# Conditioning rows in quarter strips, and a new order of loads and gathers in the opening of a conditioned block

## The chip, the cores and the metric

The kernel runs on one core of a Trainium2 chip (trn2). The core has five engines that run side by side: PE (TensorE, matrix products into PSUM), DVE (VectorE), ACT (ScalarE), POOL (GpSimd) and SP (SyncE, which here only issues transfers). Semaphores order them; sixteen DMA engines move data. The metric is the device time of one execution in microseconds (us); less is better.

## The reference, cut to what matters

x has 32 rows of 128 tokens with 512 features, fp32. `t` holds one conditioning vector of 512 per row, and `mask` marks the last tokens of each row (at most 32 of 128).

```python
m = mask[:, :, None]
emb = silu(t) @ ada_w + ada_b                      # 512 -> 3 * 512
shift, scale, gate_msa = split(emb, 3)
norm = where(m, layernorm(x) * (1 + scale[:, None]) + shift[:, None], 0)
fwd = gelu(norm @ ssm_w1 + ssm_b1) @ ssm_w2 + ssm_b2
bwd = gelu(norm @ bwd_w1 + bwd_b1) @ bwd_w2 + bwd_b2     # the two flips cancel
x = x + gate_msa[:, None] * where(m, fwd + bwd, 0)
shift_mlp, scale_mlp, gate_mlp = split(silu(t) @ ffada_w + ffada_b, 3)
h = gelu_tanh((layernorm(x) * (1 + scale_mlp) + shift_mlp) @ ff_w1 + ff_b1)   # 512 -> 1024
out = x + gate_mlp[:, None] * (h @ ff_w2 + ff_b2)
```

The first half (the lines with ssm and bwd) changes only masked tokens; the second half runs over all 4096.

## The kernel before, in words

**First half, over slots.** The masked tokens are numbered, and the first 512 become slots, four tiles of 128. `find_slots` (products with `rank` at L238, then DVE) gives the token of every slot, `gather` (L254) fetches the tokens' rows of x into `xc[0]` to `xc[3]` by indirect transfers on POOL. `pick` is a 0/1 matrix of batch rows by slots, repeated in four strips of 32 partitions. A tile goes through `statistics` (L155, with a root on POOL), `modulated` (L182, L183), four transposes on PE (L190), eight blocks f of the hidden layer (L582 for the first tiles, L199 for the rest; f0 to f3 use ssm_w1, f4 to f7 bwd_w1), and `project` (L216) with w2. `finish_slots` (L320 to L324) writes the new rows of tiles 0 and 1 to `x1_wide` in DRAM, with their own mean and root. Tiles 2 and 3 follow later as `xn_late`, `xT_t`, hidden "s1", and projections s2 and s3.

**Conditioning.** `modulation_matmuls` (L279) multiplies silu(t), transposed (`sT`, 512 by 32), with `ada_a` in four blocks k of 128 rows. The results for shift, scale and gate lie in three strips of 32 partitions (one batch row each) and 512 columns. The gate's own product is made as four partial strips (`gate_strips`, L541), copied by ACT, and added up by one product with `strips` (L550); L541 then runs once more, as `pm_keep_clock`, and its result is not used. `of_slots` (L299) spreads a kind from batch rows to a slot tile by a product with `pick`; its output is 128 by 512 in one PSUM bank. `keep_gate` copies gates to SBUF. The second half's conditioning is `pm_f` from `ada_f`, transposed into `modT` (L727).

**Second half, over all tokens.** 32 tiles in four pairs of sides, each side four tiles. For the first pair, `raw[0]` to `raw[3]` (two tiles each) hold x; `own_statistics` (L168 to L172) computes mean and root; `take_first_half` (L752) overwrites the rows that the first half changed, by eight indirect transfers from `x1_wide` with out-of-range indices skipped. `normalised_of_side_0` and DVE's 32x32 transposes make side 0 ready for `turned` (L832, transfers that finish the transpose); `normalised_of_side_1` makes four tiles for `turn(0)` to `turn(3)` (PE transposes at L821, DVE L813). Both products of the second half use Strassen's scheme with seven products on halves, at two levels; `weight_sums` (L639) and `combine` (L342) make the sums of weight blocks, `token_sums` (L922 to L932) those of activations. PE's products are at L993 (first layer) and L1180 (second layer).

**Order.** From L384 on all five engines run in program order. SP issues nearly all loads (its queue is in order too); POOL issues indirect ones; ACT issues a few. `load_behind_gathers` (L134) puts a one-element memset on POOL ahead of a load, so that SP issues that load only once POOL has issued what stands before the memset. Around the change PE's order is: pm_ss for k = 0 to 2, find_slots(1), pm_ss for k = 3, L541, L299, L550, L541, transposes, hidden. PSUM has pools ps_t (two banks), ps_h (three) and ps_o (three); a tile of a pool waits for the last reader of the tile whose bank it takes. `after` (L1252 to L1262) lists what is put behind which hidden block of "s1"; `put` does the same in the second half.

## Time and profile before

| what | value |
|---|---|
| runs | 463.61, 465.93, 467.93 us, median 465.93 |
| profiled execution | 468.7 us, span 467.0 us |
| busy: PE, DVE, ACT, POOL | 450.4, 339.2, 176.7, 156.3 us |
| mean granted clock of PE | 0.992 |
| DMA | 70.95 MB, 152 GB/s over the span |
| loads of the opening in SP's order | ada_a 4 x 512 KB, ada_a gates 1 MB, w1 2 x 1 MB, raw 4 x 512 KB, w2 2 x 1 MB, biases, fw1 2 MB, ada_f 4 x 768 KB |
| fw2 (2 MB) | issued by SP at 96.94 us |

The profile is of one execution. Its page gives the busy time of each engine, of 40 equal slices, the chain of waits that ended last, and groups of instructions by line; the trace behind it can be asked for the timeline or for the busy time in any stretch. PE's weight loads are a row of their own (PEld) and overlap its products. An fp32 product is recorded as two instructions, so a count of eight is four products.

### The profile page before, as it was taken

What the parts mean: (1) busy time and instruction counts of PE and PEld (TensorE: products, weight loads), DVE (VectorE), ACT (ScalarE), POOL (GpSimd) and SP (SyncE); (2) the same over time, 40 slices, a digit from 0 to 9 for tenths busy, and PEclk for the clock granted to TensorE, in tenths of its full rate; (3) what the DMA queues carried; (4) which work ended last, traced back from release to release, by engine and by line L of the source; (5) the groups of instructions that cost most, each with busy time, mean ns of one, the idle gap of its engine ahead of it and who ended that gap; (6) DMA issues with size and microseconds to landing.
All of it is one profiled execution on the core that took longest, in us unless ns stands there. A gap on an engine that the chain in (4) does not pass through costs nothing.

```text
span 467.0 us, 5898 instructions
## 1 busy us (share of the span) xinstructions
PE 450.4 (96%) x2034; PEld 366.2 (78%) x2034; DVE 339.2 (73%) x549; ACT 176.7 (38%) x381; POOL 156.3 (33%) x147
## 2 busy tenths in 40 slices
PE   6799999999899999999999999999999999999995
PEld 2186467578688888888888888888888887888884
DVE  4688767879979857996687389967873986433645
ACT  3032023544255173254544623544546144562000
POOL 4220052038774000289720004897000025660000
PEclk9799999999999999999999999999999999999999
DMA  7999336984404661934067429330773342213022
GB/s 278 363 392 392 134 76 113 340 302 175 157 1 185 98 125 41 341 111 162 3 208 103 96 78 331 108 136 2 221 107 80 125 168 80 79 66 116 0 79 105
DMA packets 82755, 70.95 MB, mean 152 GB/s; under 512 B 63136, under 2 KB 63664, under 8 KB 81698
## 3 DMA queue, kind: packets, MB, share of 16 engines
q1 hardware_dynamic: 67874, 58.47, 39.9%
q0 software_dynamic: 4064, 10.54, 6.3%
q10 hardware_dynamic: 10784, 1.52, 2.2%
q8 instruction: 17, 0.28, 0.2%
q14 instruction: 16, 0.13, 0.1%
HBM read 56.84 MB, written 13.70 MB: 151 GB/s over the span
## 4 chain that ended last, share of the span: by engine, by line
PE 75%; DVE 9%; DMA 4%; SPq 4%; ACT 3%; POOL 3%; issue 2%; ACTq 0%; DVEq 0%; POOLq 0%
PE a_o L1180 17%; PE a_m L993 15%; PE e_o L1180 13%; PE e_m L993 12%; PE po_s L216 6%; PE ph_s L199 5%; SPq L832 3%; DMA ada_a<-in_L_cond_ada_w_dram 3%; PE part_s L299 2%; DMA xT<-xn 1%; DVE sx L922 1%; ACT xT L815 1%; PE ph_s L582 1%; DVE t L342 1%; PE pm_f L279 1%
## 5 line engine op out<-in xcount | busy, mean ns | idle before, releaser
L1044 POOL TENSOR_TENSOR ha<-p_m,ha 128x512 f32<-128x512 f32 x20 | 25.8, 1290 | 176.4 <-ACT ha L1051 167.2
L1180 PE MATMUL e_o<-fw,ha 128*128 128x256 f32 x256 | 57.9, 379 | 0.0
L815 ACT ACTIVATE xT<-xT,modT 128x128 f32<-128x128 f32 x112 | 44.2, 479 | 33.3 <-DMA xT<-xn 31.0
L1180 PE MATMUL a_o<-t,hb 128*128 128x256 f32 x240 | 54.1, 379 | 0.0
L1180 PEld LDWEIGHTS e_o<-fw,ha 128*128 128x128 f32 x256 | 48.6, 190 | 6.6
L1180 PEld LDWEIGHTS a_o<-t,hb 128*128 128x128 f32 x240 | 45.6, 190 | 6.2
L955 ACT ACTIVATE hb<-hb,biasT 128x256 f32<-128x256 f32 x64 | 29.0, 500 | 28.9 <-POOL hb L1077 19.4
L1007 ACT COPY p_m<-e_m 128x512 f32<-128x512 f32 x27 | 15.8, 586 | 49.8 <-PE e_m L993 49.8
L1044 POOL TENSOR_TENSOR hb<-p_m,hb 128x512 f32<-128x512 f32 x20 | 29.3, 1467 | 1.5 <-DVE hb L1023 1.2
L752 POOL DMA_INDIRECT x<-x_rows,slot_i x24 | 27.6, 1150 | 6.3 <-issue 5.4
L1180 PE MATMUL a_o<-fw,ha 128*128 128x256 f32 x128 | 29.0, 380 | 0.0
L1180 PE MATMUL e_o<-fw,s 128*128 128x256 f32 x128 | 28.9, 379 | 0.0
L1180 PE MATMUL a_o<-t,s 128*128 128x256 f32 x128 | 28.9, 379 | 0.0
L1051 ACT COPY ha<-e_m 128x512 f32<-128x512 f32 x32 | 18.5, 579 | 25.8 <-PE e_m L993 25.3
L216 PE MATMUL po_s<-w,h_s 128*128 128x512 f32 x64 | 28.3, 592 | 0.0
L1180 PEld LDWEIGHTS a_o<-fw,ha 128*128 128x128 f32 x128 | 24.2, 190 | 3.5 <-ACT a_o L1119 0.2
L1180 PEld LDWEIGHTS e_o<-fw,s 128*128 128x128 f32 x128 | 24.3, 190 | 3.3
L1180 PEld LDWEIGHTS a_o<-t,s 128*128 128x128 f32 x128 | 24.3, 190 | 3.3
L955 ACT ACTIVATE ha<-e_m,biasT 128x256 f32<-128x256 f32 x48 | 20.1, 469 | 16.0 <-PE e_m L993 14.9
L1018 DVE TENSOR_TENSOR e_m<-a_m,ha 128x512 f32<-128x512 f32 x20 | 13.9, 696 | 16.4 <-POOL ha L1044 6.6
L993 PE MATMUL e_m<-s,fw 128*128 128x256 f32 x92 | 23.8, 382 | 1.0 <-DVE e_m L1018 1.0
L993 PE MATMUL a_m<-xT,tw 128*128 128x256 f32 x96 | 24.6, 379 | 0.0
(228 smaller groups left out, 896.4 us busy)
## 6 DMA issues: line engine op xcount, KB each, us to landing
tw<-t_rows SPq DMA_DIRECT2D x16, 896.0 KB, 4.6
x<-in_x_dram SPq DMA_DIRECT2D x16, 512.0 KB, 6.4
gate<-gate_rows POOLq DMA_DIRECT2D x8, 1024.0 KB, 5.1
out_dram<-x SPq DMA_DIRECT2D x15, 512.0 KB, 3.3
xT<-xn SPq DMA_DIRECT2D x92, 64.0 KB, 2.3
fw<-in_L_cond_ff_w_dram SPq DMA_DIRECT2D x2, 2048.0 KB, 15.4
ada_f<-in_L_cond_ffada_w_dram SPq DMA_DIRECT2D x4, 768.0 KB, 16.6
ada_a<-in_L_cond_ada_w_dram SPq DMA_DIRECT2D x4, 512.0 KB, 3.6
```

Of the source, the lines that this page charges most:

```text
L199: nc.tensor.matmul(ph[:, :n], w[:, k, ts(f, P)], xT[:, k, :], start=(k == 0), stop=(k == KC - 1))
L216: nc.tensor.matmul(po, h[f][:, ts(i, P)], w[:, f, :], start=(f == 0), stop=(f == HC - 1))
L752: nc.gpsimd.indirect_dma_start(out=raw[i // 2][:, i % 2] if p == 0 else xs[i // G][i % G // 2][:, i % 2], out_offset=None, in_=x1_rows if ...
L815: nc.scalar.activation(out, src, AF.Identity, bias=shift, scale=scale)
L832: queues[(b + q // 2) % len(queues)].dma_start(dst[ts(q, R), b], src[ts(b, R), q])
L955: nc.scalar.activation(dst[:, n], src[:, n], AF.Gelu_apprx_tanh, bias=biasT[:, f : f + 1])
L993: nc.tensor.matmul(bank[:, ts(n, QT)], self.w_block(j, product)[:, ts(n, P)], self.x_block(j, product), start=(product in ("P1", "P5") and ...
L1007: nc.scalar.copy(p5, e)
L1018: nc.vector.tensor_tensor(e, a, p5, add)
L1044: nc.gpsimd.tensor_tensor(self.place(RESULT[j], c), self.p5[j], other, ALU.add)
L1051: nc.scalar.copy(self.place(RESULT[j], c), src)
L1180: nc.tensor.matmul(part, src[:, k, ts(i, P)], w[product][:, k, :], start=(last and k == 0), stop=True, skip_group_check=True,)
```

## The change

It has five parts.

1. **Strips by quarter of the features.** The conditioning is laid out with the four strips of 32 partitions as four quarters j of 128 features, and shift, scale and gate side by side in each (`mod1`, `mod2`: 128 by 3 by 128). `modulation_matmuls` runs four products per block k, each with as many columns as kinds times 128. `of_slots` yields four banks, one for each quarter, for one or more slot tiles and kinds. `modulated_by_strips` therefore runs eight DVE instructions of 128 columns in place of two of 512. `gates_of_slots` makes all four tiles' gates at once, with four ACT copies. The bias loads become one of 64 KB for each kind, in rows of 512 bytes.
2. **Opening order.** ada_a's gate columns load behind the second gather; the first part of w1 between the two; the bias of shift and scale between ada_a's blocks 1 and 2; raw[2] and raw[3] behind fw1. The gate's products run behind the first tile's hidden blocks, f0 to f3 of both tiles are run tile by tile, and the own statistics of raw[0], raw[1] and of raw[2], raw[3] move to two later places.
3. **PE fed in the opening.** Four bf16 products of zeros at the start, and products into `pm_keep_clock` after the blocks k = 0 and 1 and after the first `of_slots`.
4. **Second-layer weights.** fw2 is loaded in eight parts, each behind one gather of `take_first_half(0)`; combine(0, 1) of fw2 runs on POOL behind weight_sums(4).
5. **Smaller moves.** token_sums(1, 0) and (1, 1) run ahead of the first product; fw1's combines are split around finish_slots(0); gate_rows is written by four transfers; some small tiles move to another SBUF pool. The loop for masked tokens beyond the slots is changed in the same manner.

```diff
+    def load_ada(t, w, blocks, width):
+
+        for k in blocks:
+            nc.sync.dma_start(t[:, k, :width], w[ts(k, P), :width])
+
+    def load_conditioning_bias(t, vec, kinds, queue):
+
+        rows = vec.rearrange("(m j c) -> m j c", m=3, c=P)
+        for m in kinds:
+            queue.dma_start(t[:, m], rows[m].unsqueeze(1).to_broadcast([KC, B, P]))
...
+    ada_a = adap.tile([P, KC, 3 * D], F32, tag="ada", name="ada_a")
+    load_ada(ada_a, ada_w, range(2), 2 * D)
+    load_conditioning_bias(modb_a, ada_b, range(2), nc.sync)
+    load_ada(ada_a, ada_w, range(2, KC), 2 * D)
...
     def modulation_matmuls(pm, ada, lo, hi, blocks):
+        kinds = ada.rearrange("p k (m d) -> p k m d", d=D)
         for k in blocks:
-            for j in range(lo, hi):
+            for j in range(KC):
                 nc.tensor.matmul(
-                    pm[ts(j, B), :],
+                    pm[ts(j, B), : (hi - lo) * P],
                     sT[:, k, :],
-                    ada[:, k, ts(j, D)],
+                    kinds[:, k, lo:hi, ts(j, P)],
                     start=(k == 0),
                     stop=(k == KC - 1),
                 )
 
     def modulation_rows(pm, mod, modb, lo, hi):
-        rows = slice(lo * B, hi * B)
-        nc.vector.tensor_tensor(mod[rows], pm[rows], modb[rows], ALU.add)
...
+        view = pm[:, : (hi - lo) * P].rearrange("p (m c) -> p m c", c=P)
+        nc.vector.tensor_tensor(mod[:, lo:hi], view, modb[:, lo:hi], ALU.add)
+
+    def of_slots(picked, tiles, mod, kinds, banks, name):
+
+        n = kinds.stop - kinds.start
+        t = [
+            pool.tile([P, 512], F32, tag=tag, name=f"{name}_{j}")[:, : len(tiles) * n * P].rearrange(
+                "p (a m c) -> p a m c", m=n, c=P
+            )
+            for j, (pool, tag) in enumerate(banks)
+        ]
+        for at, c in enumerate(tiles):
+            for j in range(KC):
+                nc.tensor.matmul(
+                    t[j][:, at],
+                    picked[ts(j, B), ts(c, P)],
+                    mod[ts(j, B), kinds],
+                    start=True,
+                    stop=True,
+                )
+        return t
...
+
+    def modulated_by_strips(src, strips, at, t, mean, rstd):
+
+        for j in range(KC):
+            nc.vector.scalar_tensor_tensor(
+                t[:, ts(j, P)], src[:, ts(j, P)], mean, strips[j][:, at, 1], ALU.subtract, ALU.mult
+            )
+        for j in range(KC):
+            nc.vector.scalar_tensor_tensor(
+                t[:, ts(j, P)], t[:, ts(j, P)], rstd, strips[j][:, at, 0], ALU.mult, ALU.add
+            )
+        return t
...
+
+    def gates_of_slots(tiles):
+
+        strips = of_slots(
+            pick, tiles, mod1, slice(2, 3), 2 * [(ps_o, "o")] + 2 * [(ps_t, "tr")], f"gate_s{tiles[0]}"
         )
...
-        return t
+        t = ssm.tile([P, len(tiles), D], F32, tag="gs", name=f"gs_{tiles[0]}")
+        for j in range(KC):
+            nc.scalar.copy(t[:, :, ts(j, P)], strips[j][:, :, 0])
+        return [t[:, n] for n in range(len(tiles))]
...
-        def combine(self, *which):
+        def combine(self, *which, engine=nc.vector):
 
             for j in which:
                 out, x, y = self.sums[j]
-                nc.vector.tensor_tensor(out, x, y, ALU.subtract)
+                engine.tensor_tensor(out, x, y, ALU.subtract)
...
+    zeros = tp.tile([P, 512], BF16, tag="t", name="zeros")
+    nc.vector.memset(zeros, 0.0)
+    pm_keep_clock = ps_h.tile([P, 512], F32, tag="h", name="pm_keep_clock")
+    for _ in range(4):
+        nc.tensor.matmul(pm_keep_clock, zeros[:, :P], zeros, start=True, stop=True)
...
-    broadcast_rows(modb_a, ada_b, nc.scalar)
...
+    load_conditioning_bias(modb_a, ada_b, (2,), nc.scalar)
...
-    gather_slots(find_slots(0))
+    token_i = find_slots(0)
+    both = xp.tile([P, 2, D], F32, tag="x", name="xc_0")
+    xc += [both[:, c] for c in range(2)]
+    gather(xc[0], token_i[:, 0:1])
     load_behind_gathers(w1[:, :, :D], ssm_w1)
-    load_behind_gathers(w1[:, :, D:], bwd_w1)
+    gather(xc[1], token_i[:, 1:2])
+    load_behind_gathers(ada_a[:, :, 2 * D :], ada_w[:, 2 * D :])
+    load_blocks(w1[:, :, D:], bwd_w1)
     raw = [x_tile(2 * n, 2) for n in range(2 * G // 2)]
     x_of = {0: [[t[:, :, :D] for t in raw[2 * side : 2 * side + 2]] for side in range(2)]}
-    for n, t in enumerate(raw):
-        nc.sync.dma_start(t[:, :, :D], x[2 * n : 2 * n + 2].rearrange("b s d -> s b d"))
+
+    def load_raw(n):
+        nc.sync.dma_start(raw[n][:, :, :D], x[2 * n : 2 * n + 2].rearrange("b s d -> s b d"))
+
+    load_raw(0)
+    load_raw(1)
     load_blocks(w2[:, :KC], ssm_w2)
     load_blocks(w2[:, KC:], bwd_w2)
...
-    mod1 = const.tile([3 * B, D], F32, name="mod1")
-    nc.vector.tensor_scalar(modb_a[B : 2 * B], modb_a[B : 2 * B], 1.0, None, ALU.add)
+    mod1 = const.tile([P, 3, P], F32, name="mod1")
+    def keep_clock(n, k):
+        for _ in range(n):
+            for j in range(KC):
+                nc.tensor.matmul(
+                    pm_keep_clock[ts(j, B), : 2 * P],
+                    sT[:, k, :],
+                    ada_a[:, k, ts(j, 2 * P)],
+                    start=True,
+                    stop=True,
+                )
+
     pm = ps_o.tile([P, 512], F32, tag="o", name="pm_ss")
-    modulation_matmuls(pm, ada_a, 0, 2, range(KC - 1))
+    for k in range(KC - 1):
+        modulation_matmuls(pm, ada_a, 0, 2, (k,))
+        if k < 2:
+            keep_clock(1, k)
     token_i = find_slots(1, (ps_h, "h"))
     modulation_matmuls(pm, ada_a, 0, 2, range(KC - 1, KC))
+    nc.vector.tensor_scalar(modb_a[:, 1], modb_a[:, 1], 1.0, None, ALU.add)
     modulation_rows(pm, mod1, modb_a, 0, 2)
...
+    strips = of_slots(pick, (0, 1), mod1, slice(0, 2), 3 * [(ps_o, "o")] + [(ps_h, "h")], "part_s0")
+    keep_clock(3, 0)
...
+    xn_s = []
+    for c in range(2):
+        mv, rstd = statistics(xc[c : c + 1], f"s{c}")
+        if c == 0:
+            gather_slots(token_i)
+        xn_s.append(modulated_by_strips(xc[c], strips, c, xn[:, c], mv[:, 0, 0:1], rstd))
...
+    load_raw(2)
+    load_raw(3)
+    ada_f = adap.tile([P, KC, 3 * D], F32, tag="ada", name="ada_f")
+    modb_f = adap.tile([P, 3, P], F32, tag="modb", name="modb_f", bufs=1)
+    load_ada(ada_f, ffada_w, range(KC), 3 * D)
+    load_conditioning_bias(modb_f, ffada_b, range(3), nc.sync)
...
+        if c == 0 and f % 2 == 0:
+            t = ps_h.tile([P, 512], F32, tag="h", name=f"ph_s0_{f}")
+            for n in range(2):
+                ph_s[f + n] = t[:, ts(n, NH)]
...
-    hidden_of_tile(0, 0)
-    hidden_of_tile(1, 0)
+    for f in range(KC):
+        hidden_of_tile(f, 0)
     transposed_slots(xn_s[1], xT_s[:, :, ts(1, P)], "s1")
-    hidden_of_tile(2, 0)
+    pm = ps_o.tile([P, 512], F32, tag="o", name="pm_g")
+    modulation_matmuls(pm, ada_a, 2, 3, range(KC))
+    modulation_rows(pm, mod1, modb_a, 2, 3)
...
+    totals = const.tile([P, 2], F32, name="totals")
+    nc.vector.tensor_copy(totals, pt[:, :2])
...
-    for n, t in enumerate(raw):
-        own_statistics(t, 2, f"x_{n}")
...
-    for f in range(3):
+    for f in range(KC):
         hidden_of_tile(f, 1)
...
+        for done in (f - 1, f) if f % 2 else ():
+            t = ssm.tile([P, NH], F32, tag="h", name=f"h_s0_{done}", bufs=HC)
+            nc.scalar.activation(t, ph_s[done], AF.Gelu, bias=biasT[:, done : done + 1])
+            h1.append(t)
...
+    gs = gates_of_slots(range(NC))
+    strips = of_slots(
+        pick, (2, 3), mod1, slice(0, 2), 3 * [(ps_o, "o")] + [(ps_t, "tr")], "part_s2"
+    )
+    xn_late = [
+        modulated_by_strips(
+            xc[2 + c], strips, c, spare[1][:, c], mv_t[:, c, 0:1], rstd_t[:, c : c + 1]
         )
-
-    gs = []
-    gate_and_next_tile(0)
+        for c in range(2)
+    ]
+    for n in range(2):
+        own_statistics(raw[n], 2, f"x_{n}")
+    h1 += hidden(xT_s, NH, w1, 0, AF.Gelu, "s0", ssm, range(KC, HC - 1))
...
+    for c in range(2):
+        with_gated_bias(c, gs[c])
...
-    h1 += hidden(xT_s, NH, w1, 0, AF.Gelu, "s0", ssm, range(3, HC - 1))
-    gate_and_next_tile(1)
-    Weights(fw1, KC // 2, FF // 2, t_1).combine(0, 1, 2, 3)
-    with_gated_bias(1, gs[1])
+    fw1_of = Weights(fw1, KC // 2, FF // 2, t_1)
     h1 += hidden(xT_s, NH, w1, 0, AF.Gelu, "s0", ssm, range(HC - 1, HC))
+    fw1_of.combine(0, 1)
     finish_slots(0, h1, gs[0])
+    fw1_of.combine(2, 3)
     t = in_blocks(group_of_tiles("tw_3"))
     t_sum[3] = [t[:, :4], t[:, 4:]]
     weight_sums(3)
     store_weight_sums(3)
-    nc.vector.tensor_scalar(modb_f[B : 2 * B], modb_f[B : 2 * B], 1.0, None, ALU.add)
...
-    mod2 = const.tile([3 * B, D], F32, name="mod2")
-    pm = ps_o.tile([P, 512], F32, tag="o", name="pm_f")
+    nc.vector.tensor_scalar(modb_f[:, 1], modb_f[:, 1], 1.0, None, ALU.add)
+    mod2 = const.tile([P, 3, P], F32, name="mod2")
+    pm = ps_h.tile([P, 512], F32, tag="h", name="pm_f")
     modulation_matmuls(pm, ada_f, 0, 3, range(KC))
     modulation_rows(pm, mod2, modb_f, 0, 3)
+    for n in range(2, 4):
+        own_statistics(raw[n], 2, f"x_{n}")
...
+        for m in range(2):
+            nc.tensor.transpose(ptr[:, ts(m, P)], mod2[:, m], ident)
+        nc.vector.tensor_copy(
+            modT.rearrange("p k (m b) -> p m k b", b=B),
+            ptr[:, : 2 * P].rearrange("p (m k b) -> p m k b", m=2, b=B),
+        )
...
+            if behind:
+                behind(i)
...
-    take_first_half(0, x_of[0], range(2 * G))
+    def load_fw2_part(k):
+        load_behind_gathers(fw2[:, k : k + 1], ff_w2[ts(k, P)])
+
+    take_first_half(0, x_of[0], range(2 * G), load_fw2_part)
...
-    nc.gpsimd.dma_start(gate_rows, mod2[2 * B : 3 * B, :])
+    for j in range(KC):
+        nc.gpsimd.dma_start(gate_rows[:, ts(j, P)], mod2[ts(j, B), 2])
...
+    def combine_behind_weight_sums():
+        done = stp.tile([1, 1], F32, tag="done", name="done", bufs=1)
+        nc.gpsimd.tensor_copy(done, t_sum[4][1][0:1, 2, 0:1])
+        fw2_of.combine(0, 1, engine=nc.gpsimd)
...
-    after[0] = [second_gates, transposed_modulation]
+    after[0] = [transposed_modulation]
...
+        combine_behind_weight_sums,
...
-    nc.sync.dma_start(fw2, ff_w2.rearrange("(k p) f -> p k f", p=P))
+    for n in range(2):
+        now.token_sums(1, n)
...
-    for n in range(2):
-        now.token_sums(1, n)
...
-            put(4, 1, fw2_of.combine, 0)
-            put(4, 3, fw2_of.combine, 1)
```

## The prediction

> **What bounds the kernel now.** I read the busy times by stretch first, then the chain of waits, then the timeline where PE is not full. In the stretches the columns are the stretch, then busy time (and count) of PE, PE's weight loads, DVE, ACT and POOL, the granted clock, the DMA share and GB/s.
>
> ```profile
> 0.00:24.60 24.60, 17.44 (x64) 5.75 (x65) 13.00 (x36) 4.91 (x8) 8.15 (x21) 0.86 0.91 325
> 24.60:92.00 67.40, 67.39 (x290) 42.78 (x291) 54.31 (x107) 19.35 (x41) 14.05 (x16) 1.00 0.71 237
> 92.00:131.00 39.00, 35.17 (x157) 28.93 (x156) 34.88 (x53) 15.26 (x31) 25.07 (x20) 1.00 0.57 202
> 131.00:386.00 255.00, 254.92 (x1179) 222.91 (x1178) 197.00 (x298) 116.28 (x259) 86.99 (x72) 1.00 0.46 129
> ```
>
> PE is full from 24.6 to 92 and from 131 to 386 us. It idles 7.2 us in the opening, 3.8 between 92 and 131, and 5.5 after 386, which the change does not touch. So there is something to win in three ways: an earlier first hidden-layer product, less PE work, and the 3.8 us. The chain of waits (start, us, what) shows the opening:
>
> ```profile
> 3.15 11.86 DMA ada_a<-in_L_cond_ada_w_dram
> ...
> 15.14 1.06 PE pm_g L541 x8
> 16.20 3.71 PE part_s L299 x8
> ...
> 24.61 2.02 PE ph_s L582 x16
> ```
>
> The scale and shift rows are done at 13.4, but their spreading to slots (L299) stands in PE's queue behind pm_g, which waits for the last part of ada_a. PE then runs at half clock (mean 0.54, 0.50, 0.50, 0.75 in the 2 us stretches from 16 to 24). The next lines are POOL's and PE's timeline (start, us, instruction, idle before and its releaser):
>
> ```profile
> 62.84 1.24 POOL L752 DMA_INDIRECT x<-x_wide,slot_i  x1 [3.76 <-DMA x_wide<-t_s]
> ...
> 72.57 1.00 POOL L752 DMA_INDIRECT x<-x_wide,slot_i  x1 [0.30 <-issue]
> ...
> 118.78 4.10 DVE L342 TENSOR_TENSOR t<-fw 128x1024 f32<-128x1024 f32 x1
> ...
> 123.54 1.13 PE L993 MATMUL a_m<-xn_sy,tw 128*128 128x256 f32 x4 [2.24 <-DVE hb L1023]
> ```
>
> Eight gathers 1.39 us apart fill side 1's tiles. DVE has the last one normalised at 76.2, and PE starts turn(0) at 76.56, just in time. The combine at 118.78 takes 4.10 instead of 1.22 us and leaves PE idle for 2.24.
>
> **What the Trainium skill says.** "TensorE: Matmul & The Clock Gate", Part 1: the clock halves after an idle window of 3.4 us and returns after a busy one. The trace agrees: pm_ss's first eight records take 3.41 us and four later ones 1.05, so full rate came near 9.7; half follows from 16.1 after a stretch with little work, and full near 23, about two windows apart each. Its Part 3: matmuls in different row or column groups run together. Agrees: pm_g's four of 512 take 1.06 us together, where L216's single ones take 0.86 each. "SBUF — State Buffer", Who interferes with whom: a DVE instruction with two SBUF inputs is locked out while a GpSimd instruction reads SBUF. Agrees: the 4.10 us combine ends at 122.88, one run of 1.22 after the tensor_tensors that POOL began at 119.32 and 120.54 (until 121.79).
>
> **The change part by part.** *Opening.* Each pm_ss block drops from 0.85 us (two 512-wide matmuls together) to 0.43 (four 256-wide). Two bias loads go into SP's queue before ada_a's blocks 2 and 3: two issues at 0.5 us (L119's 0.34 to 0.58 each) and 128 KB, 0.35 us at 370 GB/s. In exchange ACT's queue carries 64 KB instead of 192 KB, so I cost the landing at nothing; the cover for the issues is that DMA is busy with blocks 0 and 1 (1 MB, 2.8 us) meanwhile, and without it up to 1.3 us goes onto the first product. L531 no longer holds DVE for the bias (1.1 us), so rows are done at 12.5. The strips follow at once: 8 matmuls, 0.45 us for each slot tile, ready at 13.3. The first gather took 6.5 us to land beside saturated DMA; with ada_a's last 1 MB moved behind it I take 4.5 (bounds 2.7, the gathers of 62 us, and 6.5), so 12.3. Statistics cost 1.05 (12.5 to 13.6). The two 512-wide products (1.63 us for both) become eight of 128. Nearest row: L813, 128x128 from PSUM, 8 in 2.63 us, 0.33 each; bounds 0.25 and 0.40. That is 2.7, so xn_s0 at 16.5 instead of 19.9. From there to the first hidden product were 1.35 us (23.23 to 24.58): **17.9 instead of 24.6**. The four zero matmuls lie before the mask lands (2.8) and cost nothing. keep_clock(1, k) lies before block 2's landing (9.98; up to 0.85 each if that comes sooner), keep_clock(3) (1.3 us) before 16.5. Whether the clock holds is open: 0 to 1.7 us.
>
> *Loads.* The bytes are the same, the order is new. ada_a's gate part (1 MB) now follows the second gather and w1's first half on SP: at 370 GB/s from 9.4, with two gathers (0.5 MB) beside them, it lands near 18, and pm_g reads it at 22.4. Raw tiles 2 and 3 go behind fw1, so w2, the biases and fw1 land 2.7 us sooner; the tiles land before 45 and are read at 57. Cover gone, each would stop PE or DVE for its own lateness; 4 to 12 us of room make me take nothing.
>
> *PE up to the projection.* Before: 17.5 us from 24.6 to 42.1. After: hidden f0 to f3 for both tiles, 8 x 0.99 = 7.9; transposes 0.6; pm_g moved here 1.1; counts 0.1; gates (16 matmuls of 128, four together) 1.1. Then a new wait: part_s2 needs two of ps_o's three banks and one of ps_t's that the gates fill, so PE stands until ACT has copied three gate strips (three of L309's 0.59, behind two Gelus of 0.48), with its own 0.9 some 2.8 together. Hidden f4 to f7: 7.1. Sum 20.7, so projection at 38.6: the lead shrinks from 6.7 to 3.5. Queued behind the waiting matmuls are those four hidden blocks, and DVE waits for the strips. Then pm_f falls from 3.56 to 2.6, the second gates (1.91) go, ptr_mod loses 0.25. PE reaches turn(0) at **70.4 instead of 76.6**.
>
> *DVE and the gathers.* DVE has no such lead. It idles until the strips (29.2), then: late tiles 6.2 with the banks' waits; two own statistics 3.6 (1.81 each); b2 0.7; two gated biases 2.9; counts 1.4; combine(0,1) 2.5; finish 0 2.5; combine(2,3) 2.5; weight sums 2.2; finish 1 2.5. That ends at 56.2, where before it was 58.4. Then modb_f and rows 0.7 and, new ahead of the gathers, the statistics of raw tiles 2 and 3, 3.6, whose root POOL must do before its gathers: 61.4 instead of 62.84 (x_wide lands earlier, 60.7). Between gathers POOL now has a memset (0.23 at L135): 1.58 apart, the eighth at 72.5. It needs 4.0 to turn(0) as before, plus 0.6 for 2 MB of fw2 beside it (bounds 0 and 3.8, the opening's landing). **turn(0) at 77.1 instead of 76.6.** SP issues the first half's turned rows behind the eight weight parts, at 74.4 instead of 72.1; ACT's 83.2 becomes 85.5, and PE needs the first scaled halves (88.7) only after 92, which covers it by 3.3 us. The weight sums' six stores follow on SP, 2.3 later too, against a first read of t_rows at 94.85. gate_rows becomes four issues (2.3 us of POOL), covered by POOL's idle time to 99. Moving token sums costs nothing: DVE idles from 94.4 to 96.6.
>
> *Clock.* PE idles 6.7 us before turn(0). That holds a whole idle window, so about 3.4 us of busy work runs at half rate: **+1.7** (0 to 2.6).
>
> *92 to 131.* The combine on DVE goes to POOL (two of 1024, about 2.5 each, from L1044's 1.27 for 512). POOL is free at 80 to 85, where DVE reads PSUM, and its next operation with two SBUF inputs comes at 86. PE's 2.24 goes, and most of 0.58 and 0.96 with the two token sums moved ahead: **-3.3** (-1.5 to -3.8).
>
> **Sum:** +0.5 + 1.7 - 3.3 = -1.1 us. The profiled execution took 468.7 (span 467.0); the median of the runs is 465.93, so 464.8.
>
> **Rivals.** *The lead gets through:* strips at 0.25 each and the first gather early (16.5 for the first product) start the gathers 2.7 earlier, memsets hide in the 0.30 issue gap (1.39 apart), turn(0) at 72.5 and no half clock: -4.1 - 3.8 = -7.9, 458. For it: every row I took is the dearer of two; against: L813 is the same shape from PSUM. *Slower:* fw2's parts between the gathers. 256 KB more every 1.58 us makes some 328 GB/s, near the opening's 325 to 400, where gathers took 6.5 us. Then turn(0) comes at 80.6 (+4.1), the clock costs 2.6, fw2 lands late, and POOL's combine locks DVE out, leaving only -1.5: +5.2, 471.1. It decides from a landing of about 6 us. Against: it is under the highest rate seen. *The array is not kept at work:* half clock through the first hidden products as from 16 to 23 before; 1.7 more on the DVE chain and turn(0), 466.5.
>
> **Numbers.** Gathers bind, as summed: 0.44, own range 460.6 to 470.0 (ends of turn(0) -1.5 to +3, clock and 92 to 131). Lead gets through 0.32; slower 0.19; clock not held 0.05. A measurement here tells about 1% from no change: 461.3 and 470.6. Of the first case 0.05 lies below 461.3. Faster 0.37, same 0.44, slower 0.19. The range 457 to 472 takes in the rivals' centres.
>
> **What would show it.** First hidden product near 18; ACT's three copies before part_s2 on PE; DVE full from 29 to 61; gathers 1.6 apart; PE idle 5 to 7 us before turn(0), then 0.5 clock; no wait at the old combine. I am wrong if PE does not wait at turn(0), or if gathers land after 6 us.

## The result, and the profile after

| | before | after |
|---|---|---|
| median of 20 runs each | 465.48 us (463.61 to 469.18) | 466.50 us (465.15 to 467.88) |
| ratio after to before | | 1.0009, 95% interval 0.9988 to 1.0031 |
| profiled execution, its span | 468.7, 467.0 us | 467.88, 466.2 us |
| busy PE, DVE, ACT, POOL | 450.4, 339.2, 176.7, 156.3 us | 451.3, 334.5, 175.4, 164.3 us |

The interval of the ratio takes in 1: no change that can be measured. The 20 runs of before fall into two groups, 12 from 463.61 to 465.93 us and 8 from 467.93 to 469.18, with the profiled execution (468.7) at the level of the second, while the runs of after all lie between 465.15 and 467.88, the profiled one being the slowest; so these two profiles are compared with each other first, and with others further below.

After, busy time by stretch (columns as in the prediction: PE, PE's weight loads, DVE, ACT, POOL with counts, granted clock, DMA share, GB/s), with two more stretches:

```profile
0.00:24.60 24.60, 21.27 (x170) 12.36 (x174) 13.04 (x48) 4.71 (x8) 8.04 (x21) 1.00 0.88 313
24.60:92.00 67.40, 61.92 (x316) 40.22 (x305) 51.63 (x116) 18.43 (x41) 23.06 (x30) 0.95 0.82 262
92.00:131.00 39.00, 38.38 (x168) 31.43 (x167) 33.05 (x56) 15.76 (x31) 24.55 (x21) 1.00 0.47 166
131.00:386.00 255.00, 254.98 (x1180) 223.19 (x1179) 197.46 (x299) 115.61 (x257) 86.62 (x72) 1.00 0.47 129
70.00:80.00 10.00, 4.76 (x15) 2.62 (x14) 7.02 (x13) 0.95 (x2) 5.82 (x13) 0.83 0.99 201
80.00:92.00 12.00, 12.00 (x35) 5.94 (x34) 8.32 (x20) 8.22 (x19) 4.79 (x3) 0.85 0.94 287
```

PE works more in the opening and idles only 0.6 us between 92 and 131 (3.8 in the kernel before). But it has lost what it had before: the full stretch from 24.6 to 92. It stands 5.2 us between 70 and 80 and then runs at a lower clock. The chain of waits (start, us, what) of the kernel after shows why:

```profile
13.30 0.44 DVE mod L296
...
13.78 2.13 PE part_s L309 x16
...
19.93 3.81 PE ph_s L626 x32
...
30.23 0.57 ACT gs L337
...
30.84 2.10 PE part_s L309 x14
32.95 7.10 PE ph_s L205 x32
40.05 13.73 PE po_s L222 x32
...
54.66 2.76 PE pm_f L286 x32
...
57.44 0.56 DVE mod L296
58.00 0.61 DVE st_x L174
...
73.16 4.05 DMA x<-x_wide,slot_i
...
78.31 3.41 PE po_s L222 x4
...
95.99 0.86 PE a_m_alone L1038 x4
```

The first hidden product starts 4.7 us earlier than in the chain of before (19.93 for 24.61), the projection (40.05) only 2.1 earlier. Behind the projection, which ends at 53.8, it stays on PE for pm_f until 57.4 and then leaves PE: DVE's rows of pm_f (`mod`) wait for it, and the own statistics of raw[2] and raw[3], their root on POOL and the eight gathers follow. It returns to PE at 77.83. The finish of tile 1 and x_wide are not on it. The next two projection products (four records) take 3.41 us at half rate instead of 1.72. The timeline there (start, us, instruction, idle before and its releaser):

```profile
57.50 0.32 SPq L351 DMA_DIRECT2D x_wide<-t_s  x1
...
61.70 1.07 POOL L178 TENSOR_TENSOR x<-x,half 128x2 f32<-128x2 f32 x1 [1.10 <-DVE x L177]
62.94 1.72 POOL L795 DMA_INDIRECT x<-x_wide,slot_i  x1 [0.16 <-POOL x L178]
...
64.67 0.09 POOL L139 MEMSET fw<- 1x1 f32 x1
...
73.16 1.00 POOL L795 DMA_INDIRECT x<-x_wide,slot_i  x1 [0.21 <-issue]
...
73.74 0.33 PE L866 MATMUL ptr<-ident,xn 128*128 128x128 f32 x1 [2.13 <-DVE xn L820]
...
74.76 4.16 ACTq L877 DMA_DIRECT2D xT<-xn  x2
...
77.83 0.47 PE L866 MATMUL ptr<-ident,xn 128*128 128x128 f32 x1 [1.65 <-DVE xn L820]
...
80.28 2.35 POOL L370 TENSOR_TENSOR t<-fw 128x1024 f32<-128x1024 f32 x1 [0.18 <-DMA xT<-xn]
```

The account of the two profiles, after minus before in us at each mark: first hidden product -4.7; projection -2.1; store of x_wide -1.6 (57.50 for 59.11); first gather +0.1 (62.94 for 62.84); last gather +0.6; last transpose of turn(0) ended +1.1; first product of the second half +3.8 (95.82 for 92.05 in the timelines); second layer's first product -0.5 (136.69 for 137.18); span -0.8. So 3.8 us are lost up to the first product of the second half, and 4.3 are won from there to the second layer's first (40.87 us for 45.13).

### The profile page after: what moved, and what is told of

Read it like the earlier page. It is cut to its first block, busy times and chain, and to the rows that moved or that the text cites. A ratio compares the mean times of both kernels' runs of the same rounds, so it can differ in the third digit from the quotient of the medians.

```text
span 466.2 us, 6213 instructions
## 1 busy us (share of the span) xinstructions
PE 451.3 (97%) x2162; PEld 372.4 (80%) x2162; DVE 334.5 (72%) x571; ACT 175.4 (38%) x380; POOL 164.3 (35%) x161
## 4 chain that ended last, share of the span: by engine, by line
PE 89%; DVE 3%; issue 2%; POOL 2%; DMA 1%; ACT 0%; POOLq 0%; DVEq 0%
PE a_o L1225 23%; PE a_m L1038 19%; PE e_o L1225 18%; PE e_m L1038 15%; PE po_s L222 6%; PE ph_s L626 2%; PE ph_s L205 2%; POOL x L795 1%; PE part_s L309 1%; DMA x<-x_wide,slot_i 1%; PE last L1225 1%; PE a_m_alone L1038 1%; PE pm_f L286 1%; PE ptr L866 0%; DVE s L977 0%
## 5 line engine op out<-in xcount | busy, mean ns | idle before, releaser
L222 PE MATMUL po_s<-w,h_s 128*128 128x512 f32 x64 | 30.6, 631 | 0.0
L1096 ACT COPY ha<-e_m 128x512 f32<-128x512 f32 x32 | 18.5, 579 | 25.8 <-PE e_m L1038 25.3
L1038 PE MATMUL a_m<-xT,tw 128*128 128x256 f32 x96 | 24.6, 379 | 0.0
```

The costliest lines, as they stand in the source:

```text
L222: nc.tensor.matmul(po, h[f][:, ts(i, P)], w[:, f, :], start=(f == 0), stop=(f == HC - 1))
L1038: nc.tensor.matmul(bank[:, ts(n, QT)], self.w_block(j, product)[:, ts(n, P)], self.x_block(j, product), start=(product in ("P1", "P5") and ...
L1096: nc.scalar.copy(self.place(RESULT[j], c), src)
```

## The experiments

All ratios are to the kernel before, run on the same chip in the same session. The edits are to the changed kernel, whose own ratio is 1.0009, save in e8 and e12.

**The turns later** (e1_turns_late), so that PE does both projections while the gathers land.

```diff
-        turn(0),                     # in after[7]
-    po_s2 = project(0, h1, w2, "s2", {2: turn(1), 4: turn(2), 6: turn(3)})
...
-    of_x[0].one(1)                   # now behind s3
+    po_s2 = project(0, h1, w2, "s2")
...
-    po = project(1, h1, w2, "s3", bank=(ps_h, "h"))
+    po = project(1, h1, w2, "s3", {2 * k: turn(k) for k in range(KC)}, bank=(ps_h, "h"))
```

> The changed kernel, with turn(0) to turn(3) moved from the end of the hidden layer and projection s2 into projection s3, so that PE does the 13.8 us of projection while the gathers land. Theory (the lead ends in PE's wait for the gathers): the 5.2 us of idle time between 71.6 and 77.8 and the 2.6 us of half clock go; s3 ends near 88, and the first product of the second half starts at 89 (the first scaled halves of side 0 are there at 88.7) instead of 96.0; DVE's sums of side 1 come 4 to 5 us later than PE then and take some of it back: span 460 to 463 against 466.2. Rival (what stands behind the turns binds as well: turned rows of side 0, DVE's sums, the stores of the weight sums): first product at 94 or later, span 465 to 467.

Ratio 1.0045 (1.0025 to 1.0064), a loss of 0.45%, and the span of the profile, 467.1, lies above what both theories expected. Timeline:

```profile
75.07 4.04 ACTq L877 DMA_DIRECT2D xT<-xn  x2
...
79.22 0.47 ACT L209 ACTIVATE h_s<-ph_s,biasT 128x256 f32<-128x256 f32 x1 [3.84 <-DMA xT<-xn]
...
79.75 1.77 PE L222 MATMUL po_s<-w,h_s 128*128 128x512 f32 x2 [2.96 <-ACT h_s L209]
...
92.18 1.03 PE L1038 MATMUL a_m_alone<-xT,fw 128*128 128x256 f32 x4
...
100.80 2.07 PE L1038 MATMUL e_m<-s,fw 128*128 128x256 f32 x4 [3.27 <-DVE e_m L1063]
```

Six products fill the wait, then the seventh needs a Gelu that stands on ACT behind its turned rows: ACT's issue of two took 4.04 us. The first product of the second half is 3.6 us earlier than in the changed kernel, yet DVE, whose sums now come later, stops PE for 3.27 at 100.8, and the four records behind that wait take 2.07 us, half rate, instead of 1.03. Neither theory had the Gelus.

**Unused products in the wait** (e2_unused), **own statistics moved** (e3_raw01, e4_raw0123).

```diff
+        for _ in range(7):           # ahead of turn(0)
+            nc.tensor.matmul(t, xT_t[:, 0, :P], w2[:, 0, :], start=True, stop=True)
```

> The changed kernel, with seven products of 512 columns, whose result is not used, on PE ahead of turn(0) (7 x 0.86 = 6.0 us, 71.6 to 77.6). Theory (half clock after the wait costs 2.6 us): last transpose stays at 77.8 to 78.3, the four projection products behind it take 1.9 instead of 3.6 us, first product near 93.4, span 463.5 to 464.5. Rival (the clock's loss is given back later, or the time after the wait is set by DVE or DMA): first product earlier by less than 1 us, span 466.

```diff
+    for n in range(2):               # e3, e4: was behind xn_late
+        own_statistics(raw[n], 2, f"x_{n}")
     gs = gates_of_slots(range(NC))
...
+    for n in range(2, 4):            # e4 only: was behind modulation_rows of pm_f
+        own_statistics(raw[n], 2, f"x_{n}")
     total, start_at, more_i, col_l = count_more()
```

> The changed kernel, with the own statistics of raw[0] and raw[1] (3.6 us of DVE) moved ahead of the gates, into the 5.1 us in which DVE waits for the strips. Theory A (projection on PE, which ends at 53.8, sets finish 1, and DVE's full stretch from 32.6 to 57 only ties with it): finish 1 starts at 53.9 to 54.3 as now, first gather at 62.5 to 63, turn(0) as now, span 465.5 to 466.7. Theory B (the prediction's: the chain of DVE sets finish 1): x_wide, gathers and turn(0) all 3.6 us earlier, no half clock, span 460 to 462.

> As the kernel before it in this list, and in addition the own statistics of raw[2] and raw[3] from behind finish 1 to behind the gated biases, where the first move has made room. Theory A (projection sets finish 1; behind it the two statistics and their root hold the first gather, which x_wide alone would let start near 61.2): first gather at 61.0 to 61.4 instead of 62.9, turn(0)'s last transpose at 76.1 instead of 77.8, half clock 1 to 2.6 us still paid: span 463.5 to 465. Theory B (the chain of DVE sets everything): 5 us or more earlier, span 459 to 461. Rival C (statistics so early wait for raw[2] and raw[3] to land, after 39): DVE idles there, finish 0 and 1 later, span 467 or more.

e2: 0.9977 (0.9953 to 1.0002), an interval that overlaps with the changed kernel's, so the gain is read from the profile. The two products (four records) behind turn(0) take 1.88 instead of 3.62 us and the clock is 1.00 from 70 to 92. Its first hidden product came at 17.98, 1.95 earlier than in the changed kernel's profile; with that taken off, the first product of the second half is 2.5 earlier: the clock's price.

```profile
91.39 1.03 PE L1038 MATMUL a_m_alone<-xT,fw 128*128 128x256 f32 x4
```

Of this lead of 4.4 us the span (464.8) keeps 1.4: some 1.8 us are lost again in waits between 176 and 206, and the rest was not traced.

e3: 0.9998 (0.9978 to 1.0017), and its profile settles the question. From the first transpose behind the projection to the first gather are 9.33 us (50.99 to 60.32), where the changed kernel has 9.32 (53.62 to 62.94), though DVE now idles 2.82 us ahead of finish 0:

```profile
44.33 0.69 DVE L348 TENSOR_TENSOR t_s<-po_s,gs 128x512 f32<-128x512 f32 x1 [2.82 <-PE po_s L222]
...
54.81 0.56 DVE L296 TENSOR_TENSOR mod<-pm_f,modb_f 128x384 f32<-128x384 f32 x1 [0.87 <-PE pm_f L286]
```

So PE sets the first gather, as theory A said, and not the chain of DVE. But it does so less through finish 1 than through pm_f, which stands on PE behind the projection and for which DVE waits in both kernels (0.87 us here, 0.53 in the changed kernel). The span is 463.6 because the opening got its clock sooner. PE's timeline shows it: two equal groups of eight records of 256 columns, 1.08 and then 0.61 us, and the first hidden product at 17.30:

```profile
7.15 1.08 PE L572 MATMUL pm_keep_clock<-ada_a,sT 128*32 128x256 f32 x8
...
8.83 0.61 PE L572 MATMUL pm_keep_clock<-ada_a,sT 128*32 128x256 f32 x8
...
17.30 3.81 PE L626 MATMUL ph_s<-xT_s,w 128*128 128x128 f32 x32 [0.48 <-ACT biasT L639]
```

e4: 0.9968 (0.9945 to 0.9992). The first gather now waits for x_wide itself and starts 3.8 us after its issue instead of 5.4, as theory A said; but DVE waited 2.04 for raw[2] to land at 40 (rival C):

```profile
40.07 0.69 DVE L174 BATCH_NORM_STATS2 st_x<-x 128x6 f32<-128x512 f32 x1 [2.04 <-DMA x<-in_x_dram]
...
61.23 1.69 POOL L795 DMA_INDIRECT x<-x_wide,slot_i  x1 [3.84 <-DMA x_wide<-t_s]
```

That made finish 1 late and took back all of it: from the first transpose behind the projection to the first gather are 9.8 us, 0.5 more than in the changed kernel. That the first gather falls at the time that theory A named is due to an earlier opening (first hidden product at 17.73). What makes the ratio lower than the changed kernel's is not shown.

**The second layer's weights elsewhere**: behind all gathers (e5_fw2_behind), or early (e9_fw2_early).

```diff
-    take_first_half(0, x_of[0], range(2 * G), load_fw2_part)
+    take_first_half(0, x_of[0], range(2 * G))
+    load_behind_gathers(fw2, ff_w2)  # e5; e9: load_blocks(fw2, ff_w2) behind modb_f's loads
```

> The changed kernel, with the second layer's weights as one load of 2 MB behind the eighth gather instead of eight parts between the gathers. The opening's clock comes at another time in each execution and shifts all by up to 2.6 us, so steps are read from the first gather on. Theory (the loads beside the gathers cost 1 us): gathers 1.30 apart, last gather to landing 3.1 instead of 4.05, first gather to last transpose 13.9 instead of 14.9; time 0.5 to 1.5 us below the changed kernel's 466.5. Rival (2 MB at once behind the gathers collide with the turned rows and the stores): ACT's scaled halves end after 93 instead of 91.8, or POOL's combine, which waits for the weights until some 81, runs into DVE's sums from 88 on; time equal to the changed kernel's or up to 2 us above it.

> The changed kernel, with the second layer's weights as one load behind the second conditioning's biases, where DMA is busy to 0.3 to 0.5 only (45 to 55 us), and no load and no memset between the gathers. Theory (the loads around the gathers cost 1 us at the last landing, and fill the queue in which ACT's turned rows wait): gathers 1.30 apart, last gather to landing 3.1 instead of 4.05, first gather to last transpose 13.9 instead of 14.9, ACT's last two Gelus at 74 to 78 instead of 79 and 81, first scaled half near 83.5 instead of 85.5; half clock after a wait still over 4 us remains: time 464.8 to 465.8, against 466.5. Rival (the landing is long for the gathers' own sake or for the turned rows beside it): landing near 4, time 466 to 467.

e5: 1.0034 (1.0015 to 1.0054). The last gather took 2.69 us to land, and from the first gather to the last transpose are 13.5 us instead of 14.9, so the theory on the landing holds; but the rival is right too, in its timeline:

```profile
85.07 2.34 POOL L370 TENSOR_TENSOR t<-fw 128x1024 f32<-128x1024 f32 x1 [5.85 <-DMA fw<-in_L_cond_ff_w_dram]
...
86.39 0.47 ACT L209 ACTIVATE h_s<-ph_s,biasT 128x256 f32<-128x256 f32 x1 [10.36 <-PE po_s L222]
...
86.92 7.99 PE L222 MATMUL po_s<-w,h_s 128*128 128x512 f32 x18 [0.61 <-ACT h_s L209]
...
90.15 6.26 ACT L860 ACTIVATE xT<-xT,modT 128x128 f32<-128x128 f32 x16 [0.87 <-DMA xT<-xn]
```

ACT's scaled halves end at 96.4 instead of 91.8. e9: 1.0048 (1.0031 to 1.0066). Its gathers had no load beside them, and the last still took 3.92 us to land. The first one started 7.5 us after x_wide's issue (55.19 to 62.71) instead of 5.4, the last 2.24 of them in a wait for DMA, which was busy throughout from 24.6 to 60 (share 1.02 instead of 0.82). So neither other place did better than the parts between the gathers. A landing of 3.9 us also comes without them, so they are at most a part of its cause: in the profiles of this case it is 3.7 to 4.5 us with the parts between the gathers and 2.7 to 3.9 without.

**Combine back on DVE** (e6_combine_dve), **no fill in the opening** (e7_no_fill).

```diff
-        combine_behind_weight_sums,
...
+        if p == 0:
+            put(4, 1, fw2_of.combine, 0)
+            put(4, 3, fw2_of.combine, 1)
```

> The changed kernel, with combine(0, 1) of the second layer's weights back on DVE at its two old places near 119 us, not on POOL. Theory (the prediction's: this move gives most of the 3.2 us gained between 92 and 131): PE waits there 2 to 3 us again, one combine takes 4.1 instead of 1.2 us beside POOL; time 468.0 to 469.5. Rival (the gain comes from the earlier token sums alone): PE idle below 1 us there, time 466 to 467.

```diff
-        if k < 2:
-            keep_clock(1, k)
...
-    keep_clock(3, 0)                 # and no products of zeros at the start
```

> The changed kernel without the four products of zeros and without the products behind blocks 0 and 1 and behind the strips whose results are not used. Theory (they keep the array at work): half clock reaches into the hidden products, of which 32 records take 5 to 7.4 instead of 3.8 us; projection starts 1.5 to 4 us later after the same strips; time 468 to 470. Rival (small products do not bring the clock back, and the last group only holds the transposes up by 0.5 to 1 us): first hidden product 0.5 to 1 us earlier or the same, time 465 to 467.

e6: 1.0110 (1.0088 to 1.0132). The wait is back in its timeline, to a hundredth:

```profile
118.76 4.11 DVE L370 TENSOR_TENSOR t<-fw 128x1024 f32<-128x1024 f32 x1
...
123.53 1.13 PE L1038 MATMUL a_m<-xn_sy,tw 128*128 128x256 f32 x4 [2.25 <-DVE hb L1068]
```

PE idles 2.92 us between 92 and 131 instead of 0.62, so of the 3.2 us of idle time gained there 2.3 are this move's. From the first product of the second half to the second layer's first are 43.97 us instead of 40.87, so of the 4.3 us won between these marks 3.1 are this move's; the rest falls where the token sums were moved, which was not tried by itself. The ratio says still more (1.0110 against 1.0009, some 4.7 us), and where that goes can't be read from this profile.

e7: 1.0103 (1.0083 to 1.0123). The first hidden product comes 0.6 us earlier (19.32), since the transposes no longer queue behind keep_clock(3), but its 32 records take 5.15 instead of 3.81, and the projection starts 0.7 later (40.61 for 39.89 in the timelines). Both theories hold, and the first weighs more. The profile shows only these 0.7 us of the loss; its execution took 468.29 us, less than the median of 469.22.

**The kernel before, with 2 us of PE work left out** (e8_before_less), **and unchanged** (e12_before_again).

```diff
-    after[0] = [second_gates, transposed_modulation]
+    after[0] = [transposed_modulation]
```

> The kernel before, without the second gates: the four products of 512 columns at 62.15 (1.98 us of PE) and their two copies are left out, and the late two slot tiles use the gates of the first two. Theory (PE work between the end of the projection and turn(0) lies beside x_wide and the gathers and is free to remove, and free to keep): turn(0) at the same 76.5, PE idle some 2 us ahead of it, time within 0.6 us of the kernel before (465.0 to 466.2). Rival (PE is the bound there): turn(0) and everything behind it 2 us earlier, 463.5 to 464.

> The kernel before, unchanged, for a second profile and as a measure of how far two equal kernels come out apart. The profile that the prediction rests on has half clock from 16 to 23 us; the kernel that leaves the second gates out has the same instructions up to 62 us and did not have it (eight strip records at 15.1 took 1.99 instead of 3.71 us, first hidden product at 20.2 instead of 24.6, projection at 37.6 instead of 42.0). Theory (half clock in the opening comes in some executions only, and not in most): first hidden product near 20.2, projection near 37.6, first gather near 59, turn(0) ready with a wait below 3 us and no half clock behind it, first product of the second half at 88 to 90, span 462 to 464. Rival (the opening at half clock is the rule, and the other kernel's was the exception): as the first profile, span 466 to 468. Ratio of times within 0.997 to 1.003 in both.

e8: 1.0119 (1.0082 to 1.0156): less work, and slower, where a time within 0.6 us of the kernel before's, or a shorter one, was expected. PE stands 3.8 us ahead of turn(0), and the clock falls twice (stretches, columns as above):

```profile
70.00:80.00 10.00, 6.21 (x17) 2.83 (x16) 5.96 (x14) 2.91 (x5) 1.59 (x3) 0.83 0.85 157
...
115.00:131.00 16.00, 13.75 (x57) 11.53 (x56) 14.36 (x22) 4.79 (x10) 12.52 (x10) 0.89 0.34 118
```

The theory had the wait, not the clock. Against the profile of e12, the first product behind turn(0) starts 3.1 us later (74.97 for 71.84), the first product of the second half 4.8 and the span 5.7. Not all of this is the edit's doing: the first hidden product is 0.7 later already, the gathers start 1.5 later, and the first takes 3.22 us instead of 1.45. The cause of the late gathers wasn't tried.

e12: ratio 1.0004 (0.9977 to 1.0031), profile 463.44 us, span 461.6. Its chain of waits:

```profile
13.33 1.06 PE pm_g L541 x8
14.39 1.92 PE part_s L299 x8
...
19.45 2.02 PE ph_s L582 x16
...
36.96 13.73 PE po_s L216 x32
...
71.56 0.44 PE ptr L821 x4
72.00 1.72 PE po_s L216 x4
...
87.05 0.86 PE a_m_alone L993 x4
```

Here the kernel before has no half clock from 16 to 23. The gate columns landed at 13.2 instead of 15.0, so PE waited 0.36 instead of 2.48 us ahead of L541, and everything behind is 5.2 us earlier. PE is full from 24.6 to 92. Why the columns land sooner in one execution than in another is not known.

This second profile allows a fairer comparison. Counted from the first hidden product, e3 has the marks of the changed kernel to 0.1 us, so it can stand for the changed kernel with an early clock (starts in us, from the timelines):

| | before, first profile | before, e12 | after | e3 |
|---|---|---|---|---|
| first hidden product | 24.61 | 19.45 | 19.93 | 17.30 |
| projection | 41.96 | 36.80 | 39.89 | 37.26 |
| first gather | 62.84 | 57.48 | 62.94 | 60.32 |
| first product of the second half | 92.05 | 86.89 | 95.82 | 93.13 |
| second layer's first product | 137.18 | 132.03 | 136.69 | 133.99 |
| span | 467.0 | 461.6 | 466.2 | 463.6 |

With the clock back early in both, the change wins 2.2 us in the opening, has lost them at the projection, is 6.2 us behind at the first product of the second half, and ends 2.0 us slower. The 0.8 us that it wins between the two first profiles hang on the late opening of the first one.

**Towards a better version** (e10_stats, e11_split). e10 adds the moves of own statistics to e9 (those of raw[0], raw[1] as in e3, those of raw[2], raw[3] behind the first two combines), with the third weight sums behind finish 1. e11 adds useful products in the wait to that, with the Gelus ahead of ACT's turned rows.

```diff
-    after = {4 + b: [turn_rows(b)] for b in range(4)}
+    after = {4: [], 7: [turn_rows(b) for b in range(4)]}   # turn(0) out of after[7]
...
+    po_s2 = project(0, h1, w2, "s2", {4: lambda: [turn(k)() for k in range(2)]})
+    po = project(1, h1, w2, "s3", {0: turn(2), 2: turn(3)}, bank=(ps_h, "h"))
```

> As e9_fw2_early, and in addition: own statistics of raw[0], raw[1] ahead of the gates, of raw[2], raw[3] behind the first two combines (landed by 40, as seen before), and the third weight sums behind the conditioning rows, so that nothing but finish 1 itself stands between the end of the projection and x_wide. Theory (gathers start when x_wide has landed): end of the projection to first gather 7.3 to 7.6 instead of 9.15 us; turn(0) another 1.6 to 1.9 us earlier, PE's wait near 3.4 us; time 462.8 to 464.3. Rival (the wait is then only shifted, and half clock costs the same): only the 1.7 us, 463.5 to 464.3; or DVE is now late elsewhere (weight sums stored later): 465 and above.

> As e10_stats, and in addition PE does four products of projection s2 ahead of turn(0) and turn(1), turn(2) and turn(3) go into projection s3, and ACT issues its turned rows behind the last Gelu. Theory (useful work in place of the wait, and the Gelus no longer behind the turned rows, which was what stopped the kernel with the late turns): PE idle below 1 us between 60 and 92, clock 1.00 there, first product of the second half at 88 to 90; time 458 to 461.5. Rival (DVE, which now makes its sums of side 1 after the projection, stops the first products as it did in the kernel with late turns, where 3.3 us of idle time came at 100 us and half clock with it): PE idle 3 us or more between 92 and 105, time 463 to 466.

e10: 1.0012 (0.9994 to 1.0029): from the first transpose behind the projection to the first gather 7.9 us instead of 9.3, of which x_wide's way, with fw2 ahead of it, is 4.4. Half clock stays (0.66 from 70 to 80), and the median of 465.25 us lies above what was expected. e11: 0.9953 (0.9930 to 0.9976), median 462.15 against 464.53: the lowest ratio of all and clear of the changed kernel's, though its interval overlaps with those of e2 and e4. Its stretches:

```profile
70.00:80.00 10.00, 9.13 (x31) 4.52 (x30) 7.44 (x16) 1.69 (x3) 6.65 (x8) 1.00 0.89 151
80.00:92.00 12.00, 11.39 (x42) 7.23 (x40) 11.77 (x18) 7.28 (x19) 1.28 (x1) 1.00 0.88 310
92.00:131.00 39.00, 36.50 (x168) 31.80 (x169) 31.43 (x58) 19.83 (x42) 29.27 (x25) 1.00 0.39 136
```

No long wait, no half clock, first product of the second half at 86.05. The rival names what is left: 2.48 us at 93.87, for DVE's e_m. e11 carries e9's early load, which cost 0.4% by itself; with the parts between the gathers it wasn't tried.

## Why the prediction was right, step by step

The likeliest case came true in its mechanism: the opening's lead ends in a wait at turn(0), the clock takes its share, and the stretch from 92 to 131 gives it back. The sum was -1.1 us, and the two profiles differ by -0.8.

That these lie so close is partly luck, in two ways. The terms were off by 0.6 to 1 us each and their errors cancel: turn(0) came 1.1 us later (predicted 0.5), the clock cost 2.6 (1.7), the way from there to the second layer won 4.3 (3.3), and 0.3 were won behind it. And the profile that the sum starts from had a late opening; with the clock back early in both kernels the change costs 2.0 us (e3 beside e12), and the medians moved by +1.0. The parts:

1. **Opening, first product at 17.9.** Measured 19.93: the rows were done at 13.7 instead of 12.5, the strips took 2.13 us instead of 0.9 and the last keep_clock 2.79 instead of 1.3, these two at half rate, and the transposes came 0.5 us behind xn_s0. With the clock back sooner (e3) it is 17.30. The eight DVE products took 2.16, not 2.7, and the first gather was there in time. The error lay in the other number: 24.6 is one execution's. Where the gate columns land sooner, the kernel before starts at 19.45, so at a similar clock the opening gains 2.2 us (17.30 for 19.45), not 6.7.
2. **PE up to the projection.** The new wait was named and sized: 2.75 us (30.2 to 32.95), predicted 2.8. With the gates' own work it takes back 2.6 of the lead; at a similar clock the projection of the changed kernel (37.26 in e3) is even 0.5 behind that of before (36.80 in e12).
3. **DVE's chain to finish 1** ended when predicted (56.7 for 56.2) but was not the cause: behind it DVE waited 0.53 us for pm_f, and e3 shows that 2.82 us of room in the chain win nothing. The path runs over PE, through the projection and pm_f; the prediction had no wait there. DVE was full, and it only tied.
4. **Statistics ahead of the gathers.** Right: they hold the first gather 1.6 us after x_wide (e4), at 62.94 instead of 61.4, because finish 1 ended 0.5 later, DVE then waited 0.53 us for pm_f, and POOL's root took 1.07.
5. **Gathers.** Memsets took 0.09 us and hid in the issue gap: four of the seven steps between gathers were 1.30 us, not 1.58. The landing grew by 1.0, not 0.6. That the fw2 parts alone caused it fell: it is 3.92 in e9 without them and 3.89 in e8.
6. **turn(0)** +1.1 for +0.5, **clock** 2.6 for 1.7, at the end of its range (e2: 2.5). **92 to 131** -3.2 for -3.3 in idle time, of which the combine is 2.3 (e6). Between the marks on either side it is -4.3, since the products behind each wait start slowly too (1.13 us for four records instead of 1.03), and the combine's share is 3.1.

Two of the prediction's sums are off by their own terms: PE reaches turn(0) at 70.0, not 70.4 (measured 71.6), and the slower rival's turn(0) is 80.3, not 80.6.

Of the rivals, "the lead gets through" failed at the first gather: of the lead at the projection nothing was left there. The PE work removed between the end of the projection and turn(0) (the second gates and parts of pm_f, 2.9 us) went into PE's wait for the gathers. In e12 the last tile is normalised at 71.1 and PE ready at 71.4, so 0.3 us was to be had; e8 removes 2 us of it alone, and nothing is won, though its gathers were late as well. The slow rival's landing of 6 us did not come. "The array is not kept at work" came partly: half rate to 18.5 in the profile, though without the fill it is worse (e7).

Open: what the clock's return in the opening depends on, and why the last gather takes 2.7 to 4.5 us to land.

## What to carry to other kernels

A lead in one stage is worth what the next meeting point lets through: list what else has to arrive there, and find its own chain, before adding up savings on the busy engine. Work that covers a wait also keeps the clock (e2), so taking it away can cost more than it saves, as it seems to have done in e8. Move useful work into the wait instead (e11), and check which instructions it needs are queued behind transfers on another engine. And take a second profile of the kernel before if its first is not near the median of the runs: here it would have moved every mark from the first hidden product on by 5.2 us.

## What the runs showed of the hardware

- The same instructions got full clock at different times: groups of eight 256-column records in the opening went from 1.08 to 0.61 us at 8.8 us (e3), 1.08 to 0.64 near 11.5 (e4), and in the profile after not before 18.5. The column of the granted clock reads 1.00 in all of these; the records' lengths tell it. The Trainium skill, "TensorE: Matmul & The Clock Gate", Part 1, says that the clock returns after a busy window of a free-running counter of some 3.4 us. If every full window of work counted alike, the counter's phase would shift the return by one window at most; here it moves by some 10 us, so the phase alone does not explain it, and no run shows what does.
- One pair of issues of 64 KB transposing transfers held ACT's queue for 4.16 us (after) and 4.04 us (e1) when fw2's loads were under way; pairs in the kernel before took 1.4 to 2.3 us.
- A one-element memset between two indirect transfers took 0.09 us and nothing of their spacing.
- A wait of 3.8 us ahead of turn(0), broken by single transposes of 0.33 us, left the next four records at 3.34 instead of 1.88 us (e8), and one of 5.2 us at 3.62 (after). A wait of 0.87 us at the same place left them at full rate (e11).
